# The second pass of a two-layer convolution block: normalisers, the last band's depthwise taps and the key sums in another order

## The chip, the cores and the metric

The kernel runs on one core of a Trainium2 chip. The metric is the time of one execution on the device, in microseconds. A median of three executions stands for a kernel, and a separate execution was recorded by the hardware profiler. The engines have these names in the profile: PE (TensorE, the matrix engine) and PEld (its weight loads), DVE (VectorE), ACT (ScalarE), POOL (GpSimd) and SP (SyncE, which issues most DMAs). Each engine runs its instructions in the order in which it was given them.

## The reference

Input x has 8 images of 384 channels and 64 × 64 tokens, in float32. Two layers follow each other, each with a residual (x becomes x + f(norm(x))) and each with a group normalisation of 32 groups per image in front of it.

- Layer 0 is linear attention. 1 × 1 convolutions give queries, keys and values. Queries and keys are rotated by token position and then sent through elu + 1. With 6 heads of 64 channels:

```
kv         = sum over tokens n of  k[n,d] * v[n,e]
k_sum      = sum over tokens n of  k[n,d]
out[n]     = q[n] · kv / (q[n] · k_sum + 1e-6)
layer0     = conv1x1(out, Wfc) + bfc
```

- Layer 1 is a convolutional feed-forward block. A 1 × 1 convolution is followed by a filter in the Fourier domain of every 8 × 8 block, then by a 3 × 3 depthwise convolution (zero padding), then by a gate, gelu(first half of the channels) times second half, and by a 1 × 1 convolution from 192 to 384 channels.

## The kernel before

**Tiling.** Channels lie on partitions in three tiles of 128. An image is cut into 8 bands of 512 tokens, which are 8 rows of 64. A band of an image, `x_b_j`, is loaded by SP (`load_x`), and layer 0 adds its result in place. It is stored after layer 0 (`store_x`), and POOL's queue later adds layer 1's output `y_b_j` to it in DRAM with an accumulating DMA (L845). Bands and `y` share a pool of 10 buffers, so that a load can wait for the `y` that had its buffer.

**Keys.** For each band `k_project` (matmuls pk, L438) and `v_project` (pv, L454, evicted by ACT at L461) make keys and values, and `accumulate` adds them over the tokens into one PSUM tile acc (L470; image 0 takes another form, L483).

**Second pass.** When an image's keys are complete, `queries` runs. Per band:
- `q_project` loads a table tq (SP) and does three groups of matmuls pq (L597). Then come the rotation (DVE L610, 625, 626, ACT L624) and elu + 1 (ACT L337, 338, DVE L339), which leave qc.
- `q_normalise` makes pn = q · k_sum (L635), then a chain of small steps in turn on DVE (L643, 644, 649, 651) and ACT (L648, 650): the reciprocal, split in two bf16 parts.
- `q_spread` spreads it over the channels (prb, L659, four PSUM tiles), and DVE multiplies qc by it (L668).
- `project_out` does pf (L676). DVE adds bias and residual (L680), and the sums for the next normalisation are taken on ACT and DVE.

At its start the heads' matrices are folded with the output weights (`finish`): kvt_bd on DVE (L571), pt (L583), pm (L508), mt (DVE L513). POOL copies k_sum into ks_bd (L498), which pn needs.

**Band loop.** After the second pass of image b its layer 1 runs band by band, and the keys of image b + 1 are made between its steps. `expand_filter` is pi (L694) and pd (L708), with the filter on DVE (tf, L716); `back_transform` is pb (L729), copied by ACT into a ring of two padded bands. The depthwise convolution is one ACT step (`first_taps`, L776) and eight DVE steps (`taps`, L788) per channel tile, 24 per band. `gate_taps` is L794 to L799, and `contract` is pw (L815, L826). The taps of a band run a band later, since they need the row below, and `contract` a band after that. So when image b + 1's second pass starts, bands 6 and 7 of layer 1 of image b aren't through: `before_last` contracts band 6, `gate` does the 24 taps and the gate of band 7, and `output` contracts band 7. These are called from inside `queries`, as is the chain for the next image's layer-0 normalisation and key weights (`layer0_chain(b + 1)`: small matmuls ps_m, ps_mc, ps_v, ps_r, and pbk).

**The last image** has no next keys. In bands where `on_array` holds, PE does the depthwise taps of channel tile 2 with diagonal matrices (ptap, L764), and DVE does 16 taps in place of 24.

**What sets the order.** The Python order of calls gives the order of work in outline, with generators that yield between matmul groups. A framework then schedules instructions on each engine and places the waits. There are eight PSUM buffers of 128 × 512, handed round by one pool, so a matmul group can also wait until an older tile in its buffer has been read. Two buffers hold taps.

The lines of `queries` around the normalisers and the last band's work before the change:

```
if j != 1:
    normaliser[j + 1] = q_normalise(b, j + 1, q[j + 1])
run(project)
...
q_spread(b, j, q[j], normaliser.pop(j))
if j == 0:
    gate()
```

Of the kernel before, what the change touches and what calls it, by code (L numbers as in the profile page):

```python
# [12 lines left out]
ALU = mybir.AluOpType  # L13
# [3 lines left out]
CT = 3  # L17
H = W = 64
N = H * W
NBAND = 8  # L20
# [97 lines left out]
def conv_blocks_kernel(ctx: ExitStack, tc: tile.TileContext, a: dict, out: bass.AP, nb: int):  # L118
    nc = tc.nc
# [20 lines left out]
    def load_x(b, j):  # L140
        if b >= nb:
            return
        t = xp.tile([P, CT, BT], F32, tag="x", name=f"x_{b}_{j}")
        nc.sync.dma_start(t, x_in[b][:, :, j * BT : (j + 1) * BT])
        xt[b, j] = t
# [484 lines left out]
    def q_normalise(b, j, q):  # L630

        pn = ps_tile(f"pn_{b}_{j}")
        for t in range(CT):
            for s in range(4):
                nc.tensor.matmul(  # L635
                    pn[32 * s : 32 * s + 32, :P],
                    ks_bd[:, t, :],
                    q[:, t, s * P : (s + 1) * P],
                    start=(t == 0),
                    stop=(t == CT - 1),  # L640
                )
        rn = small.tile([P, P], F32, tag="rn", name=f"rn_{b}_{j}")
        nc.vector.tensor_scalar_add(rn, pn[:, :P], 1e-6)  # L643
        nc.vector.reciprocal(rn, rn)

        part = small.tile([P, P], BF16, tag="part", name=f"part_{b}_{j}")
        parts = small.tile([P, P], BF16, tag="parts", name=f"parts_{b}_{j}")
        nc.scalar.copy(part, rn)  # L648
        nc.vector.scalar_tensor_tensor(rn, part, take_off[:, 0:1], rn, ALU.mult, ALU.add)
        nc.scalar.copy(part, rn)  # L650
        nc.vector.scalar_tensor_tensor(parts, part, take_off[:, 1:2], rn, ALU.mult, ALU.add)
        return parts
# [19 lines left out]
    def project_out(b, j, q, mt):  # L672
        for m in range(CT):
            p_ = ps_tile(f"pf_{b}_{j}_{m}")
            for t in range(CT):
                nc.tensor.matmul(  # L676
                    p_, mt[:, t, m * P : (m + 1) * P], q[:, t, :], start=(t == 0), stop=(t == CT - 1)
                )
            xm = xt[b, j][:, m, :]
            nc.vector.scalar_tensor_tensor(xm, p_, bfc[:, m : m + 1], xm, ALU.add, ALU.add)  # L680
            if m == 0:
                yield
        if j == 1:
            differences[b] = taps_pool.tile([P, CT, BT], F32, tag="dw", name=f"differences_{b}")
        band_sums(b, 1, j, xt[b, j], differences.get(b))
# [64 lines left out]

    def on_array(b, j):

        return b == nb - 1 and j in (3, NBAND - 2, NBAND - 1)

    def make_diagonals():
        t = small.tile([P, CT, C], F32, tag="wk", name="diagonals", bufs=1).rearrange("p t c -> p (t c)")
# [21 lines left out]
            dw_pe[b, j] = ps_tile(f"ptap_{b}_{j}")  # L778
            array_taps(b, j, range(9 if j == NBAND - 1 else 6))

    def taps(b, j):

        t, acc = ring[j % 2], dw[b, j]
        for m in range(CT - on_array(b, j)):
            for k in range(1, 9):
                src = t[:, m, k // 3 : k // 3 + 8, k % 3 : k % 3 + W]
                wd = w_dw[:, m, k : k + 1]
                nc.vector.scalar_tensor_tensor(acc[:, m], src, wd, acc[:, m], ALU.mult, ALU.add)  # L788

    def gate_taps(b, j):  # L790
        g = gated
# [9 lines left out]
    def depthwise_gate(b, j):  # L801
        taps(b, j)
        gate_taps(b, j)
# [43 lines left out]
    def contract(b, j):  # L847
        run(contraction(b, j))
# [14 lines left out]
    def chain_of(*chains):  # L863
        for c in chains:
            yield from c

    def run(*chains):

        chains = list(chains)
        while chains:  # L870
            chains = [c for c in chains if next(c, chains) is not chains]
# [62 lines left out]
                    sum_weight(self.wv, "wv")  # L934
                self.vbias = v_bias(self.b, self.params)

    def queries(b, keys, before_last, gate, output):


        wq, qbias = keys.wq, keys.qbias  # L940
        q, done = {}, []
        run(q_project(b, 0, wq, qbias, q))
        before_last()
        run(keys.accumulate(NBAND - 1))
        finish = keys.finish(done)
        for _ in zip(q_project(b, 1, wq, qbias, q), finish):
            pass
        prepared = []
        chain = layer0_chain(b + 1, prepared)
        normaliser = {0: q_normalise(b, 0, q[0])}  # L950
        for j in range(NBAND):

            if j < NBAND - 2:
                project = q_project(b, j + 2, wq, qbias, q)
                for _ in range(2 if j else CT):
                    next(project)
                if j == 0:
                    run(finish)
                    mt = done[0]
                if j != 1:  # L960
                    normaliser[j + 1] = q_normalise(b, j + 1, q[j + 1])
                run(project)
            if 2 <= j < NBAND - 2:
                next(chain, None)
            q_spread(b, j, q[j], normaliser.pop(j))
            if j == 0:
                gate()
            if j >= 1:
                output_ = project_out(b, j - 1, q.pop(j - 1), mt)
                if j in (1, NBAND - 2):  # L970
                    next(output_)
                    normaliser[j + 1] = q_normalise(b, j + 1, q[j + 1])
                run(output_)
                if j < NBAND - 2:
                    next(chain, None)
            if j == 2 and b < nb - 1:
                output()
            if j in (4, 5):
                load_x(b + 1, j - 4)
            if j == NBAND - 2:  # L980
                run(chain)
        run(project_out(b, NBAND - 1, q.pop(NBAND - 1), mt))
        return prepared

# [6 lines left out]
    prepared = []  # L991
    run(layer0_chain(0, prepared))
    keys = Keys(0, prepared)
# [4 lines left out]
    for c0, at, n in QRUNS:  # L998

        t, p0, quarter, first = at // P, at % P, c0 // QC, c0 % QC  # L1000
# [42 lines left out]
    def nothing():  # L1043
        pass

    before_last = gate = output = nothing
    for b in range(nb):
        prepared = queries(b, keys, before_last, gate, output)
        keys = Keys(b + 1, prepared)
        params = []  # L1050
        chain, more = norm_chain(b, 1, params), chain_of(keys.project_k(0), keys.load_values(), keys.project_k(1))
        last = b == nb - 1
        if last:

            more = contraction(b - 1, NBAND - 1) if b else iter(())
        for steps in (2, 0, 1, 1) if last else (2, 1, 1, 3):
            next(chain)
            for _ in range(steps):
                next(more, None)
        run(chain)  # L1060
        ahead = normalised(b, 0, params, (8, 8), "f")
        run(more)
        if last:
            break
        first_values = keys.project_v(0)
        next(first_values, None)
        for j in range(NBAND):
            if j < 2:
                fill = chain_of(keys.project_v(j) if j else first_values, keys.accumulate(j))
            else:  # L1070
                fill = chain_of(keys.project(j), keys.accumulate(j - 1 if j > 2 else NBAND))
            tf = []
            h = normalised(b, j, params, (8, 8), "f") if j else ahead
            store_x(b, j)
            if 1 <= j < NBAND - 1:
                load_x(b + 1, j + 1)
            layer1 = expand_filter(b, j, h, tf)
            items = 1 if j < 2 else 2

            def some(n):  # L1080
                for _ in range(n):
                    next(fill)

            next(layer1)
            some(items)
            run(layer1)
            some(2 * items)
            back_transform(b, j, tf[0])
            first_taps(b, j)
            some(items)  # L1090
            if j > 1:
                contract(b, j - 2)
            run(fill)
            keys.prepare(j)
            if j > 0:
                depthwise_gate(b, j - 1)
            stream_stats(b + 2, j)
        keys.prepare(NBAND)

        def before_last(b=b):  # L1100
            contract(b, NBAND - 2)

        def gate(b=b):
            depthwise_gate(b, NBAND - 1)

        def output(b=b):
            contract(b, NBAND - 1)


    make_diagonals()  # L1110
    b = nb - 1
    h = ahead
    for j in range(NBAND):
        tf = []
        layer1 = expand_filter(b, j, h, tf)
        run(layer1)
        store_x(b, j)
        if j < NBAND - 1:
            h = normalised(b, j + 1, params, (8, 8), "f")
        back_transform(b, j, tf[0])  # L1120
        if j and on_array(b, j - 1):

            array_taps(b, j - 1, range(6, 9))
        first_taps(b, j)
        if j >= 2:
            contract(b, j - 2)
        if j >= 1:
            taps(b, j - 1)
            gate_taps(b, j - 1)
# [45 lines left out]
```

## Time and profile before

| | |
|---|---|
| median of three executions | 3442.15 us (3442.06 to 3443.75) |
| profiled execution, own time | 3442.33 us |
| its span in the profile | 3440.6 us |
| mean granted PE clock | 0.989 |
| busy: PE, DVE, ACT, POOL | 3319.7, 2786.9, 1976.0, 143.2 us |
| chain that ended last, by engine | PE 76%, DVE 18%, ACT 4% |
| costliest group on DVE: taps, L788 | 1512 instructions, 1059.5 us |
| x load, y accumulate, tq load: issue to landing | 5.9, 7.8, 4.8 us |

The span is the time from the first to the last instruction that the profile holds, and the execution's own time is 1.73 us more. A busy time is the union of an engine's instructions; the rest of the span is idle. In lists of instructions the columns are start, duration, engine, line, operation, what it writes from what it reads, size and count of merged instructions. The bracket gives the idle time of that engine just before it and what ended it. A list of waits gives total, number and longest of them. "DVE qc L339" means: the DVE instruction of line 339 that writes qc. A matmul group's duration reaches to the modelled end of the last one, so groups overlap by a tenth or two; times per step in the text are spacings of starts.

### The profile page before, as it was taken

How to read it: one execution, taken by the hardware profiler on the slowest of the kernel's cores; microseconds unless marked ns; L12 is line 12 of the kernel's file. 1: busy time of each engine (PE TensorE's matmuls, PEld its weight loads, DVE VectorE, ACT ScalarE, POOL GpSimd, SP SyncE). 2: the span in 40 equal slices, each digit the busy share in tenths (PEclk: the TensorE clock that was granted, in tenths of full speed). 3: DMA queues.
4: the chain of work that ended last, by engine and by line, in shares of the span. 5: the costliest groups of instructions: out<-in, count | busy, mean ns of one | idle time of the engine just before them, and what ended most of it. 6: DMA issues, size and time to landing. Idle time of an engine off the chain costs nothing.

```text
span 3440.6 us, 53200 instructions
## 1 busy us (share of the span) xinstructions
PE 3319.7 (96%) x21374; PEld 1856.2 (54%) x21374; DVE 2786.9 (81%) x4430; ACT 1976.0 (57%) x3854; POOL 143.2 (4%) x247
## 2 busy tenths in 40 slices
PE   8999999999999999999999999989999899999987
PEld 5544565456654566445664456644566445664454
DVE  6587789868898688986889868897788977899597
ACT  4445666556664566555665556655576555555553
POOL 0000001000010000100001000010000000000000
PEclk9999999999999999999999999999999999999999
DMA  6323244332343333442343423334243331333112
GB/s 221 112 89 115 65 111 100 114 124 66 92 112 115 110 84 87 100 131 96 82 108 90 133 90 92 94 98 131 81 111 92 107 121 55 66 83 101 51 27 48
DMA packets 149484, 336.01 MB, mean 98 GB/s; under 512 B 27141, under 2 KB 38389, under 8 KB 141045
## 3 DMA queue, kind: packets, MB, share of 16 engines
q1 hardware_dynamic: 123844, 282.85, 24.5%
q0 software_dynamic: 25200, 49.55, 10.0%
q8 instruction: 168, 2.75, 0.3%
q14 instruction: 80, 0.65, 0.1%
q10 hardware_dynamic: 192, 0.21, 0.0%
HBM read 232.70 MB, written 99.88 MB: 97 GB/s over the span
## 4 chain that ended last, share of the span: by engine, by line
PE 76%; DVE 18%; ACT 4%; issue 1%; DMA 0%; SPq 0%; DVEq 0%; ACTq 0%
PE pi L694 14%; PE pk L438 13%; PE pf L676 13%; PE pv L454 12%; PE pq L597 7%; DVE dw L788 6%; PE pw L815 4%; PE pd L708 2%; PE pb L729 2%; PE pw L826 2%; PE acc L483 2%; PE acc L470 2%; DVE qc L339 1%; DVE qc L610 1%; ACT ring L739 1%
## 5 line engine op out<-in xcount | busy, mean ns | idle before, releaser
L788 DVE SCALAR_TENSOR_TENSOR dw<-ring,w_dw,dw 128x512 f32<-128x512 f32 x1512 | 1059.5, 749 | 262.5 <-ACT ring L745 223.9
L438 PE MATMUL pk<-wk,x 128*128 128x384 f32 x1536 | 545.0, 496 | 0.0
L676 PE MATMUL pf<-qc,mt 128*128 128x512 f32 x1152 | 518.8, 604 | 17.1 <-DVE qs L610 17.0
L597 PE MATMUL pq<-x,wq 128*128 128x512 f32 x1152 | 528.1, 607 | 0.1
L694 PE MATMUL pi<-w_in,hf 128*128 128x384 f32 x1536 | 516.1, 492 | 1.3 <-ACT hf L332 1.3
L454 PE MATMUL pv<-wv,x 128*128 128x384 f32 x1344 | 470.0, 488 | 0.0
L438 PEld LDWEIGHTS pk<-wk,x 128*128 128x128 f32 x1536 | 283.5, 191 | 205.3 <-issue 32.5
L694 PEld LDWEIGHTS pi<-w_in,hf 128*128 128x128 f32 x1536 | 287.8, 191 | 196.3 <-issue 4.6
L676 PEld LDWEIGHTS pf<-qc,mt 128*128 128x128 f32 x1152 | 214.8, 191 | 271.3 <-issue 231.8
L597 PEld LDWEIGHTS pq<-x,wq 128*128 128x128 f32 x1152 | 215.2, 193 | 255.8 <-issue 244.4
L454 PEld LDWEIGHTS pv<-wv,x 128*128 128x128 f32 x1344 | 253.6, 190 | 181.4 <-issue 8.4
L461 ACT COPY v<-pv 128x384 f32<-128x384 f32 x224 | 108.8, 486 | 417.8 <-PE pv L454 417.1
L680 DVE SCALAR_TENSOR_TENSOR x<-pf,bfc,x 128x512 f32<-128x512 f32 x192 | 141.1, 744 | 103.9 <-PE pf L676 103.2
L624 ACT ACTIVATE qs<-pq,qbias 64x512 f32<-64x512 f32 x128 | 87.6, 685 | 193.4 <-DVE qc L610 175.1
L701 ACT COPY ht<-pi 128x384 f32<-128x384 f32 x256 | 114.9, 484 | 114.7 <-PE pi L694 111.6
L815 PE MATMUL pw<-gated,w_out 128*128 128x256 f32 x768 | 177.5, 380 | 0.2 <-DVE gated L795 0.2
L441 DVE TENSOR_TENSOR kc<-pk,kbias 128x384 f32<-128x384 f32 x256 | 141.1, 551 | 40.9 <-PE pk L438 40.9
L337 ACT ACTIVATE qs<-qc 128x1536 f32<-128x1536 f32 x64 | 95.1, 1486 | 135.9 <-DVE qc L626 125.8
L845 POOL DMA_DIRECT2D out_dram<-y x63 | 80.7, 1281 | 2068.8 <-DVE dw L788 1047.8
L179 ACT ACTIVATE differences<-x,shift 128x512 f32<-128x512 f32 x168 | 120.2, 716 | 76.6 <-DVE x L680 76.6
L815 PEld LDWEIGHTS pw<-gated,w_out 128*128 128x128 f32 x768 | 145.0, 190 | 34.7 <-issue 5.7
L337 ACT ACTIVATE ks<-kc 128x1536 f32<-128x1536 f32 x64 | 95.2, 1487 | 100.9 <-DVE kc L445 72.0
(171 smaller groups left out, 4384.4 us busy)
## 6 DMA issues: line engine op xcount, KB each, us to landing
tq<-in_tq SPq DMA_DIRECT2D x64, 1024.0 KB, 4.8
x<-in_x SPq DMA_DIRECT2D x64, 768.0 KB, 5.9
tk<-in_tk SPq DMA_DIRECT2D x64, 768.0 KB, 4.4
out_dram<-x SPq DMA_DIRECT2D x63, 768.0 KB, 3.3
out_dram<-y POOLq DMA_DIRECT2D x63, 768.0 KB, 7.8
xs<-in_x SPq DMA_DIRECT2D x56, 768.0 KB, 5.9
wk<-in_wk SPq DMA_DIRECT2D x8, 576.0 KB, 3.8
wfc<-in_wfc SPq DMA_DIRECT2D x8, 576.0 KB, 7.7
```

The source lines that it names most:

```text
L179: nc.scalar.activation(out[:, m, :], x_[:, m, :], AF.Identity, bias=shift[:, m : m + 1], accum_out=of_m[0])
L337: nc.scalar.activation(e, x_, AF.Relu, scale=-1.0)
L438: nc.tensor.matmul(pk[:, :C], tokens(t), wks[:, t, :], start=(t == 0), stop=(t == CT - 1))
L441: nc.vector.tensor_add(kc[:, i, :], pk[:, :C], bias)
L454: nc.tensor.matmul(pv[:, :C], xt[b, j][:, t, i * P : (i + 1) * P], wvs[:, t, :], start=(t == 0), stop=(t == CT - 1),)
L597: nc.tensor.matmul(p_, wqs[:, t, m * P : (m + 1) * P], xt[b, j][:, t, :], start=(t == 0), stop=(t == CT - 1),)
L676: nc.tensor.matmul(p_, mt[:, t, m * P : (m + 1) * P], q[:, t, :], start=(t == 0), stop=(t == CT - 1))
L680: nc.vector.scalar_tensor_tensor(xm, p_, bfc[:, m : m + 1], xm, ALU.add, ALU.add)
L694: nc.tensor.matmul(p_[:, :C], h[:, t, i * P : (i + 1) * P], w_in[:, t, :], start=(t == 0), stop=(t == CT - 1),)
L701: nc.scalar.copy(ht[:, i, :], p_[:, :C])
L788: nc.vector.scalar_tensor_tensor(acc[:, m], src, wd, acc[:, m], ALU.mult, ALU.add)
L815: nc.tensor.matmul(p_[h][:, m - m0, :], w_out[:, 0, m * P : (m + 1) * P], gated[:, h * HT : (h + 1) * HT], start=(m == m0), stop=False,)
```

## The change

There are five parts.

1. The taps of one channel tile become a function, and the previous image's last band a generator, `last_band`: one tile's 8 taps in each of bands 2, 3 and 4 of the second pass, the gate with the third, the contraction in band 5. Before, all 24 taps and the gate were called in band 0, the contraction in band 2. In the last image's second pass the contraction is left to a later place in both kernels.
2. `queries` is written out anew. pn_1 comes after prb_0 and the first tile of pq_3, where it was right after the fold; pn_2 comes after prb_1, ahead of the second tile of pf_0. The chain's steps come up to a band later, and its rest after the loop. The loads of the next image's bands 0 and 1 come in bands 5 and 6, where they were in 4 and 5.
3. In the band loop every accumulation comes a band after its keys. Before, those of bands 0 and 1 came in their own band.
4. In the last image `on_array` holds for bands 6 and 7; before, also for band 3.
5. Band 6's last three array taps are issued in `taps`, after the contraction of band 5, where they were ahead of band 7's first taps.

```diff
     def on_array(b, j):
-        return b == nb - 1 and j in (3, NBAND - 2, NBAND - 1)
+        return b == nb - 1 and j >= NBAND - 2
...
+    def tile_taps(b, j, m):
+        t, acc = ring[j % 2], dw[b, j]
+        for k in range(1, 9):
+            src = t[:, m, k // 3 : k // 3 + 8, k % 3 : k % 3 + W]
+            wd = w_dw[:, m, k : k + 1]
+            nc.vector.scalar_tensor_tensor(acc[:, m], src, wd, acc[:, m], ALU.mult, ALU.add)
+
     def taps(b, j):
...
+        if on_array(b, j) and j < NBAND - 1:
+            array_taps(b, j, range(6, 9))
         for m in range(CT - on_array(b, j)):
...
+            tile_taps(b, j, m)
...
-    def queries(b, keys, before_last, gate, output):
+    def queries(b, keys, before_last, late):
...
-        normaliser = {0: q_normalise(b, 0, q[0])}
-        for j in range(NBAND):
-
+
+        normalise(0)
+        run(q_project(b, 2, wq, qbias, q))
+        run(finish)
+        mt = done[0]
+        q_spread(b, 0, q[0], normaliser.pop(0))
+        project = q_project(b, 3, wq, qbias, q)
+        next(project)
+        normalise(1)
+        run(project)
+        output_ = project_out(b, 0, q.pop(0), mt)
+        next(output_)
+        q_spread(b, 1, q[1], normaliser.pop(1))
+        normalise(2)
+        run(output_)
+        for j in range(2, NBAND):
             if j < NBAND - 2:
                 project = q_project(b, j + 2, wq, qbias, q)
-                for _ in range(2 if j else CT):
+                for _ in range(2):
                     next(project)
...
-                if j != 1:
-                    normaliser[j + 1] = q_normalise(b, j + 1, q[j + 1])
+                normalise(j + 1)
                 run(project)
-            if 2 <= j < NBAND - 2:
                 next(chain, None)
             q_spread(b, j, q[j], normaliser.pop(j))
-            if j == 0:
-                gate()
...
-            if j == 2 and b < nb - 1:
-                output()
-            if j in (4, 5):
-                load_x(b + 1, j - 4)
+            output_ = project_out(b, j - 1, q.pop(j - 1), mt)
             if j == NBAND - 2:
-                run(chain)
+                next(output_)
+                normalise(j + 1)
+            run(output_)
+            if j < NBAND - 2:
+                next(chain, None)
+            if j == 5:
+                load_x(b + 1, 0)
+            next(late, None)
+            if j == 6:
+                load_x(b + 1, 1)
+        run(chain)
...
+    def last_band(b):
+        for m in range(CT):
+            tile_taps(b, NBAND - 1, m)
+            if m == CT - 1:
+                gate_taps(b, NBAND - 1)
+            yield
+        if b + 1 < nb - 1:
+            contract(b, NBAND - 1)
...
-                fill = chain_of(keys.project_v(j) if j else first_values, keys.accumulate(j))
+                fill = chain_of(keys.project_v(j) if j else first_values, keys.accumulate(j - 1))
             else:
-                fill = chain_of(keys.project(j), keys.accumulate(j - 1 if j > 2 else NBAND))
+                fill = chain_of(keys.project(j), keys.accumulate(j - 1))
...
-                    next(fill)
+                    next(fill, None)
...
         back_transform(b, j, tf[0])
-        if j and on_array(b, j - 1):
-
-            array_taps(b, j - 1, range(6, 9))
         first_taps(b, j)
```

More of the change, by code (lines that the diff above doesn't have):

```diff
@@ L779, in first_taps @@
             array_taps(b, j, range(9 if j == NBAND - 1 else 6))
+    def tile_taps(b, j, m):
[4 more added lines that the diff above has]
+            nc.vector.scalar_tensor_tensor(acc[:, m], src, wd, acc[:, m], ALU.mult, ALU.add)
     def taps(b, j):
-        t, acc = ring[j % 2], dw[b, j]
+        if on_array(b, j) and j < NBAND - 1:
+            array_taps(b, j, range(6, 9))
         for m in range(CT - on_array(b, j)):
[L785 to L788, printed above, removed]
+            tile_taps(b, j, m)
     def gate_taps(b, j):
@@ L935, in prepare, with normalise @@
                 self.vbias = v_bias(self.b, self.params)
-    def queries(b, keys, before_last, gate, output):
+    def queries(b, keys, before_last, late):
         wq, qbias = keys.wq, keys.qbias
-        q, done = {}, []
+        q, done, normaliser = {}, [], {}
+        def normalise(j):
+            normaliser[j] = q_normalise(b, j, q[j])
         run(q_project(b, 0, wq, qbias, q))
@@ L949, in queries @@
         chain = layer0_chain(b + 1, prepared)
-        normaliser = {0: q_normalise(b, 0, q[0])}
-        for j in range(NBAND):
+        normalise(0)
[13 more added lines that the diff above has]
+        for j in range(2, NBAND):
             if j < NBAND - 2:
                 project = q_project(b, j + 2, wq, qbias, q)
-                for _ in range(2 if j else CT):
+                for _ in range(2):
                     next(project)
-                if j == 0:
-                    run(finish)
-                    mt = done[0]
-                if j != 1:
-                    normaliser[j + 1] = q_normalise(b, j + 1, q[j + 1])
+                normalise(j + 1)
                 run(project)
-            if 2 <= j < NBAND - 2:
                 next(chain, None)
             q_spread(b, j, q[j], normaliser.pop(j))
-            if j == 0:
-                gate()
[L968 to L975, printed above, removed]
-            if j == 2 and b < nb - 1:
-                output()
-            if j in (4, 5):
-                load_x(b + 1, j - 4)
-            if j == NBAND - 2:
-                run(chain)
+            output_ = project_out(b, j - 1, q.pop(j - 1), mt)
+            if j == NBAND - 2:
+                next(output_)
[9 more added lines that the diff above has]
+        run(chain)
         run(project_out(b, NBAND - 1, q.pop(NBAND - 1), mt))
@@ L1044, in nothing @@
         pass
-    before_last = gate = output = nothing
+    def last_band(b):
[6 more added lines that the diff above has]
+            contract(b, NBAND - 1)
+    before_last, late = nothing, iter(())
     for b in range(nb):
-        prepared = queries(b, keys, before_last, gate, output)
+        prepared = queries(b, keys, before_last, late)
         keys = Keys(b + 1, prepared)
@@ L1101, in before_last @@
             contract(b, NBAND - 2)
[L1103 to L1107, printed above, removed]
+        late = last_band(b)
     make_diagonals()
```

## The prediction

> **What bounds the kernel now.** I read the page's busy table first, then TensorE's waits, then the stage where those waits sit.
>
> ```profile
> PE 3319.7 (96%) x21374; PEld 1856.2 (54%) x21374; DVE 2786.9 (81%) x4430; ACT 1976.0 (57%) x3854; POOL 143.2 (4%) x247
> ```
>
> TensorE (PE) is idle for only 3440.6 − 3319.7 = 121 us, and no matmul of an image goes away, so this is nearly all that a reordering can win. The waits say on what PE stands:
>
> ```profile
> PE pn L635 <- DVE qc L339: 36.1, 20, 3.4
> PE pf L676 <- DVE qs L610: 17.0, 12, 1.8
> PE pb L729 <- DVE tf L716: 12.8, 7, 3.6
> PE pn L635 <- DVE qs L610: 7.9, 7, 2.3
> PE acc L470 <- ACT v L461: 6.9, 6, 1.1
> ```
>
> The normaliser (pn) and output projection (pf) lines, 36.1 + 17.0 + 7.9 = 61 us, all stand at the head of the second pass; pb is mostly the last image's. Windows of image 2 (columns: busy of PE, PE's weight loads, DVE, ACT, POOL, then clock, DMA share, GB/s) show that the other engine is then full:
>
> ```profile
> 1000.00:1060.00 60.00, 50.03 (x262) 22.39 (x257) 59.36 (x101) 30.35 (x42) 7.12 (x13) 0.97 0.31 89
> 1060.00:1120.00 60.00, 60.00 (x265) 28.53 (x266) 46.41 (x82) 32.44 (x63) 1.55 (x3) 1.00 0.47 144
> ```
>
> DVE works 59.36 of the first 60 us, then 46.41 of the next. So this is a short DVE-bound stretch before a PE-bound one. PE's timeline in it:
>
> ```profile
> 1011.16 1.05 PE L635 MATMUL pn<-qc,ks_bd 128*32 128x128 f32 x24 [0.96 <-DVE qc L339]
> 1012.14 7.99 PE L597 MATMUL pq<-x,wq 128*128 128x512 f32 x18
> 1019.97 2.10 PE L508 MATMUL pm<-wfc,kvt 128*128 128x384 f32 x6
> 1025.41 0.86 PE L635 MATMUL pn<-qc,ks_bd 128*32 128x128 f32 x24 [3.35 <-DVE qc L339]
> 1026.21 0.35 PE L659 MATMUL prb<-parts,expand 32*128 32x128 bf16 x12
> 1026.48 9.69 PE L597 MATMUL pq<-x,wq 128*128 128x512 f32 x18
> 1039.87 0.86 PE L635 MATMUL pn<-qc,ks_bd 128*32 128x128 f32 x24 [0.64 <-DVE qs L610]
> 1042.51 5.42 PE L676 MATMUL pf<-qc,mt 128*128 128x512 f32 x12 [1.78 <-DVE qs L610]
> 1054.41 0.86 PE L635 MATMUL pn<-qc,ks_bd 128*32 128x128 f32 x24 [1.34 <-DVE qc L339]
> 1059.93 7.99 PE L676 MATMUL pf<-qc,mt 128*128 128x512 f32 x18 [1.08 <-DVE qs L610]
> ```
>
> The brackets sum to 9.15 us; 0.5 of waits on kvt_bd just before and 0.17 on ps_m make 9.8. The pq group of 9.69 us, otherwise 7.9, ran partly at half clock: 1.77 us more. In the DVE timeline 16 of the 24 depthwise taps of the previous image's last band (L788) stand ahead of the elu (L339) for which pn_1 waits.
>
> **What the Trainium skill says.** "Perfetto Trace Analysis", Optimization Strategy, advises interleaving regimes when the most-contended engine changes over time; the two windows are that case. "TensorE: Matmul & The Clock Gate", Part 1, has the clock halve after at least one idle window of about 3.4 us, free-running. The trace agrees on the length (the low stretch is 3.41 us, from 1026.7), but the window before it was idle only some 2 us; the measurement decides, so I don't count gaps under 3.4 us as safe. "PSUM — Partial Sum Buffer", Specifications, gives eight banks per partition; no view shows banks, but the program has eight PSUM buffers, which decides my two new waits below.
>
> **The change, part by part** (durations are spacings in the timelines).
>
> *Last band's taps (24 × 0.66 = 15.8 us of DVE) and gate (0.6 + 2 × 0.45 = 1.5 us).* Nothing is removed. In the built order 12 taps instead of 16 now precede qc_1's elu, the other 12 and the gate follow in bands 2 to 5. DVE is thus 4 × 0.66 = 2.6 us earlier at that point, 1.26 at qc_0's elu. pn_0 hardly gains (0.3 us): POOL's ks_bd copies (L498) end at 1011.7, and their speed is untouched.
>
> *Normalisers.* pn_1 moves behind prb_0 and pq_3_0; pn_2 behind prb_1. What was queued behind pn_1's 3.35 us, the twelve prb and pq_3, goes ahead. I walked PE's new order from the same start (pq_0 at 987.04): pq_2 ends 1019.75, pm 1021.85, prb_0 1022.15. pq_3_0 now needs the buffer of pq_2_2, which ACT reads at L624 (behind its elu steps) until about 1023.6: **a new wait of 1.5 us**. pn_1 follows at 1026.35 without waiting. pq_3_1 needs a buffer of prb_0, which DVE reads at L668 until about 1029.1: **a new wait of 1.9 us**. pq_3 ends 1034.4, pf_0_0 1037.05; prb_1, pn_2 and the rest of pf_0 1043.6, pq_4's first two tiles 1048.9, pq_4 1052.5, prb_2 and pf_1 1060.6. Before, pf_1 ends at 1067.85 with 0.28 of a ps_m ahead of it that has now moved behind. So 1067.85 − 1060.6 − 0.28 ≈ **7.0 us per image**, 7 images with a predecessor: 49 us. The new waits can leave a half-clock stretch of up to 1.7 us; I take half, 0.85 × 7 = −6.
>
> *Bands 2 to 5.* There a band needs 13.2 us of DVE for its queries over 71/4 = 17.8; with 12 × 0.66 + 1.5 + 3 (layer 0's chain) = 12.4 more over four bands DVE is at (52.8 + 12.4)/71 = 92%. My walk shows no PE wait, since queries are projected two bands ahead, but DVE takes its work in order, and each late L610 holds a bank. From nothing to 3 us per image; I take 1 × 6 = −6.
>
> *contract(b,7) from band 2 to band 5.* 24 matmuls, 4.3 us of PE, all moved. Its y goes out by POOL's accumulate (7.8 us to landing). The load x_{b+1,1} takes y's buffer: issued near 1134, landing 5.9 later, 1140; pk_3_1 wants it near 1154. 13 us of cover, so nothing; without it the loss is one for one. The stores behind it on SP wait for later work anyway. x_{b+1,0} waits for an accumulate already landed: nothing.
>
> *Layer-0 chain half a band to a band later.* It ends before the keys that need wk; each small wait (0.17 to 0.3) sits elsewhere: nothing. If wk came late, pk would wait directly.
>
> *acc a band later.* In band 1 of the band loop acc stands 1.15 us on v (L461); the waits list has 6.9 us of it. The new acc_0 reads a v evicted a band earlier: **+7**. If that v were late too, the wait would return.
>
> *Image 0.* No taps precede it, PE is dense; the new bank wait costs about 0.9: **−1**.
>
> *Last image.*
>
> ```profile
> 3315.64 7.81 PE L764 MATMUL ptap<-ring,diagonals 128*128 128x512 f32 x12 [1.91 <-ACT ring L744]
> 3407.15 10.57 PE L764 MATMUL ptap<-ring,diagonals 128*128 128x512 f32 x24 [1.77 <-ACT ring L744]
> ```
>
> Band 3's tile 2 leaves the array: PE loses nine taps at (3417.56 − 3407.15)/12 = 0.87 us, where pw follows, 7.8 us in all, and the 1.91 wait, DVE gains 8 × 0.66 = 5.3, ACT one tap. Band 6's last three array taps now follow pw_5, so 3 × 0.87 = 2.6 us no longer stand between band 7's ring and its own nine. Here pb also waits for DVE's tf (2.04 and 2.50 near the end), so part of the 5.3 comes back. My walk has the end 4 to 6 us earlier; I take **+4.5**, bounds −5 (DVE sets the end throughout) and +9.7 (all of 7.8 and 1.91).
>
> Sum: 49 − 6 − 6 + 7 − 1 + 4.5 = 47.5 us. The profiled execution took 3442.33 (span plus 1.73), so 3394.8, and the median of 3442.15 lies 0.2 below: **3394.6 us**.
>
> **Rivals.** A difference from no change can be told from about 0.2% (7 us).
> *Waits only move.* The two new bank waits grow, and DVE at 92% makes others in bands 2 to 5, so that a third of the stage's 49 is left. For it: my walk already has 3.4 us of them, and DVE's work is only later, not less. Against: DVE has 13.6 us spare in the next 60. Then 7 + 4.5 − 1 + 16 = 26.5 → 3416.
> *Nothing of the second pass is won.* DVE's 120-us total bounds both windows: only acc and tail, 7 + 4.5 − 1 = 10.5 → 3432. Against: 105.8 of the 120 us are busy.
> *Slower: the last band's gate comes too late.* DVE, in order, runs it behind queries; y_7's accumulate lands after 1148, the load behind it on SP misses pk_3_1, and PE stops. It decides once y_7 slips more than 13 us against my walk; each us beyond costs one per image, six times. A slip of 25 costs 12 × 6 = 72, against the 47.5: 3467. For it: 92% leaves little to catch up. Against: a slip needs DVE over 100% for four bands.
> *The change does not do what it says:* the scheduler might hoist the spread taps again. It did hoist 12 of 24; taking it to 16 gives back about half of the stage, near 3416.
>
> **How the numbers follow.** Forecast near 3395 (its own range 3378 to 3408): 0.60. Waits move or taps hoisted, 3416: 0.20. Only acc and tail: 0.08. Slower, by the gate, the last image's −5 with clock losses, or new waits: 0.12. With no half clock and no wait in bands 2 to 5 (12 us) it is 3383, with the tail's upper bound (5 more) 3378. The range of 8 in 10 is 3374 to 3428. Faster 0.85 (the first three, less 0.03 near the bound), within 0.2% 0.05, slower 0.10.
>
> **What would show it.** Right: pn ← L339 falls from 36.1 to under 8 us; two new waits per image, pq on ACT's L624 and on DVE's L668, 1 to 2 us each; acc ← L461 gone; PE busy about as before less 8 to 14; image period from 419.7 to between 411.5 and 413.5; window 1060 to 1120 fuller on DVE, over 54. Wrong: pk waiting for x's DMA (the gate rival), pf or pq waiting on L610 in bands 2 to 5 over 2 us per image (DVE bound), low clock in each second pass, or tf late for pb throughout the last image.

## The result

The changed kernel takes 3386.34 us (median of 4 runs, 3383.77 to 3389.49), where the kernel before takes 3442.43 beside it. The ratio is 0.9837, with a 95% interval from 0.982 to 0.9854: 56 us faster. The forecast was 3394.6 with a range from 3374 to 3428, so the direction and the range held, and the gain was 8 us larger than the sum said. The profiled execution took 3384.08 us for a span of 3382.3.

The page's busy table of the changed kernel (columns as before):

```profile
PE 3300.6 (98%) x21356; PEld 1850.2 (55%) x21356; DVE 2786.1 (82%) x4438; ACT 1965.9 (58%) x3849; POOL 142.6 (4%) x247
```

PE's idle time fell from 121 to 3382.3 − 3300.6 = 82 us, and its busy time by 19 us. Some 8 of these are the nine array taps that are gone. The trace also has 53.7 us at half clock in place of 75.7; work at half speed takes twice as long, so up to 11 us of the rest is that (an estimate from these two figures). DVE works as long as before. PE's list of waits (total, times, longest) has new names at its head:

```profile
PE pq L597 <- ACT qs L624: 16.9, 7, 2.5
PE pb L729 <- DVE tf L716: 13.3, 7, 2.8
PE pq L597 <- DVE qc L668: 11.0, 7, 2.0
PE px L400 <- DMA x<-in_x: 7.2, 3, 6.4
PE pn L635 <- DVE qc L339: 6.8, 7, 1.0
```

The normaliser's wait on the elu (L339) went from 36.1 us to 6.8, those of pf and pn on L610 and that of acc on L461 are no longer in the list. In their place stand exactly the two that the forecast named: pq on L624 and on L668, once in each of seven images. The same stage of image 2 in PE's timeline:

```profile
1001.49 1.05 PE L635 MATMUL pn<-qc,ks_bd 128*32 128x128 f32 x24 [0.96 <-DVE qc L339]
1002.47 7.99 PE L597 MATMUL pq<-x,wq 128*128 128x512 f32 x18
1010.30 2.10 PE L508 MATMUL pm<-wfc,kvt 128*128 128x384 f32 x6
1012.33 0.44 PE L659 MATMUL prb<-parts,expand 32*128 32x128 bf16 x12
1015.26 2.84 PE L597 MATMUL pq<-x,wq 128*128 128x512 f32 x6 [2.50 <-ACT qs L624]
1018.04 0.86 PE L635 MATMUL pn<-qc,ks_bd 128*32 128x128 f32 x24
1020.94 7.11 PE L597 MATMUL pq<-x,wq 128*128 128x512 f32 x12 [2.04 <-DVE qc L668]
```

After these two waits PE's next one is 0.2 us at a ps_r in the band loop. The windows that answer to those shown of before, moved by the same distance from pq_0:

```profile
990.48:1050.48 60.00, 54.00 (x266) 24.18 (x262) 57.30 (x93) 29.00 (x40) 7.12 (x13) 0.97 0.39 121
1050.48:1110.48 60.00, 60.00 (x263) 27.73 (x261) 54.79 (x95) 36.58 (x69) 0.14 (x1) 1.00 0.29 98
```

DVE's crowded window fell from 59.36 to 57.30 and the next rose from 46.41 to 54.79, with PE full in it: this is the interleaving of the two stretches.

Where the 58.2 us of span went can be read from the start of one image's pq_0 to the next one's (before, after):

| part | before | after | gain |
|---|---|---|---|
| up to pq_0 of image 0 | 159.6 | 158.9 | 0.8 |
| image 0 | 407.75 | 406.36 | 1.4 |
| images 1 to 6, sum | 2516.9 | 2477.2 | 39.7 |
| image 7 to the end of its second pass | 154.5 | 149.6 | 5.0 |
| image 7, rest | 201.8 | 190.4 | 11.4 |

An image of the changed kernel takes 412.3 us (images 1, 3, 5 and 6) or 414.0 (2 and 4), against 419.7 (image 6: 418.5). The 1.7 us go with one stretch of half clock in the second pass. The second pass alone, from pq_0 to the end of the last pf, takes 163.9 us before and 158.7 after, as the mean of images 1 to 6. That is 31.5 of their 39.7 us; the other 8.2 lie in the band loop.

### The profile page after: what moved, and what is told of

The parts are those of the page before. It is cut to its first block, busy times and chain, and to the rows that moved or that the text cites. A ratio compares the mean times of both kernels' runs of the same rounds, so it can differ in the third digit from the quotient of the medians.

```text
span 3382.3 us, 53235 instructions
## 1 busy us (share of the span) xinstructions
PE 3300.6 (98%) x21356; PEld 1850.2 (55%) x21356; DVE 2786.1 (82%) x4438; ACT 1965.9 (58%) x3849; POOL 142.6 (4%) x247
## 4 chain that ended last, share of the span: by engine, by line
PE 82%; DVE 14%; ACT 2%; issue 1%; DMA 0%; SPq 0%; DVEq 0%; ACTq 0%
PE pf L676 15%; PE pk L438 14%; PE pi L694 13%; PE pv L454 13%; PE pq L597 9%; DVE dw L787 6%; PE pw L820 4%; PE pb L729 3%; PE pd L708 2%; PE pw L831 2%; PE acc L470 2%; PE acc L483 2%; PE pn L635 1%; DVE qc L610 1%; DVE qc L339 1%
## 5 line engine op out<-in xcount | busy, mean ns | idle before, releaser
L461 ACT COPY v<-pv 128x384 f32<-128x384 f32 x224 | 108.7, 485 | 423.9 <-PE pv L454 416.3
L624 ACT ACTIVATE qs<-pq,qbias 64x512 f32<-64x512 f32 x128 | 87.4, 683 | 123.8 <-DVE qc L610 122.6
```

## Experiments

Two theories were to be told apart. The first: the gain comes from DVE work (the last band's taps and gate) that leaves the crowded head of the second pass. The second: it comes from the normalisers' places on PE. Parts 3 to 5 of the change were measured on their own; the chain's steps and the loads of part 2 were not. The indented texts say what was expected of a run before it was built.

### The last band early again

```diff
         for m in range(CT):
             tile_taps(b, NBAND - 1, m)
-            if m == CT - 1:
-                gate_taps(b, NBAND - 1)
-            yield
+        gate_taps(b, NBAND - 1)
+        yield
...
         q_spread(b, 0, q[0], normaliser.pop(0))
+        next(late, None)
...
-            next(late, None)
+            if j == 2:
+                next(late, None)
```

> The changed kernel (3386 us) with the last band's 24 taps and gate called in band 0 of the second pass again and its contraction in band 2, the normalisers staying in their new places. If the gain of the second pass (6.2 us per image without the accumulation's 1.1) comes from DVE work taken out of its crowded head, 9 of the 24 taps and the gate, about 8 us of DVE, come back between the first elu steps and pf_0: nearly all is lost, 7 images x 5 to 6, 3420 to 3428. If it comes from the normalisers' places alone, 3384 to 3392. I expect most of it lost, 3415 to 3425.

It takes 3426.6 us (0.9953 of the kernel before, 0.9936 to 0.997): 40 us are lost, 5.8 per image on average. PE's timeline of it:

```profile
1022.74 4.54 PE L597 MATMUL pq<-x,wq 128*128 128x512 f32 x6 [2.49 <-ACT qs L624]
1027.20 0.86 PE L635 MATMUL pn<-qc,ks_bd 128*32 128x128 f32 x24
1028.41 5.42 PE L597 MATMUL pq<-x,wq 128*128 128x512 f32 x12 [0.35 <-DVE qc L668]
1037.55 0.35 PE L659 MATMUL prb<-parts,expand 32*128 32x128 bf16 x12 [1.14 <-DVE parts L651]
1040.20 1.51 PE L635 MATMUL pn<-qc,ks_bd 128*32 128x128 f32 x24 [2.30 <-DVE qs L610]
1053.88 0.86 PE L635 MATMUL pn<-qc,ks_bd 128*32 128x128 f32 x24 [0.73 <-DVE qc L339]
```

The waits are back, behind pn_1 instead of at it: DVE has eight taps and the gate between the elu of band 2 and the end of band 3's rotation, and the steps of the second normaliser (L643 to L651) stand among them. In the second passes of images 1 to 7 PE idles 61.9 us in place of 38.4, and half clock is granted for 47.8 us in place of 13.6, which is up to 17 us of PE's work (an estimate, half of the difference). These two make up the 40 us. The mean second pass of images 1 to 6 takes 164.5 us, no less than the 163.9 of the kernel before: new places for the normalisers don't help while this work stands there. The edit moves the contraction back too; in image 2's second pass PE has no wait of over 0.1 us behind those shown, so the contraction's place costs nothing there.

### The normalisers in their old places

```diff
-        q_spread(b, 0, q[0], normaliser.pop(0))
-        project = q_project(b, 3, wq, qbias, q)
-        next(project)
         normalise(1)
-        run(project)
+        q_spread(b, 0, q[0], normaliser.pop(0))
+        run(q_project(b, 3, wq, qbias, q))
+        q_spread(b, 1, q[1], normaliser.pop(1))
         output_ = project_out(b, 0, q.pop(0), mt)
         next(output_)
-        q_spread(b, 1, q[1], normaliser.pop(1))
         normalise(2)
```

> The changed kernel with pn_1 right after the fold again and pn_2 after the first pf_0, the taps staying spread. The elu for which pn_1 waits starts 36.3 us after the pass begins in the changed kernel and 36.5 before, so pn_1 would again stand some 3 us. If the normalisers' places make the gain, it is lost, 3415 to 3428; if the taps do, PE loses the 3 us at pn_1 but not the two new waits of 2.5 and 2.0 us on ACT L624 and DVE L668, since these buffers come free meanwhile: 3380 to 3392. I expect the second, up to 3395.

It takes 3398.2 us (0.9872, 0.9857 to 0.9886), 12 us more than the changed kernel, some 3 us above the range I gave. PE's waits in it:

```profile
PE pn L635 <- DVE qc L339: 29.5, 14, 3.4
PE pf L676 <- ACT y L845: 10.7, 6, 1.8
```

pn_1 stands 3.35 us on the elu as before, and neither L624 nor L668 is waited for. What was not foreseen is the second line: band 5's pf waits for ACT to move y out of the contraction's buffers, 1.8 us in six images. That the PSUM buffers are handed on in another order is the likely reason; no view shows the buffers. With this wait PE idles 44.7 us in the second passes of images 1 to 7, in place of 38.4, and half clock is granted for 30.7 us in place of 13.6, up to 8.5 us of PE's work (an estimate, as above).

The four orders side by side, as the mean second pass of images 1 to 6, in us:

| | normalisers in their old places | in their new places |
|---|---|---|
| taps and gate early | 163.9 (before) | 164.5 |
| taps and gate spread | 160.7 | 158.7 (changed) |

So the first theory holds for the larger part: spreading the taps wins 3.2 us per image with the old places and 5.8 with the new ones. The new places win 2.0, and only once the taps are spread. The kernel before also differs from the others in the places of the chain and of two loads.

### Accumulation a band later, alone

```diff
-                fill = chain_of(keys.project_v(j) if j else first_values, keys.accumulate(j))
+                fill = chain_of(keys.project_v(j) if j else first_values, keys.accumulate(j - 1))
             else:
-                fill = chain_of(keys.project(j), keys.accumulate(j - 1 if j > 2 else NBAND))
+                fill = chain_of(keys.project(j), keys.accumulate(j - 1))
```

This is made in the kernel before, and the filling loop passes over an empty chain.

> The kernel before with the accumulations of bands 0 and 1 a band later and nothing else. If v, a band old by then, is always there, the 1.15 us of PE at acc go in six images: 6.9 us, 3435 to 3436. If the second pass stays DVE-bound, so that PE's gain in the band loop is only waited off in front of pn, no change, 3441 to 3443.

It takes 3433.0 us against 3442.9 (0.9973, 0.9963 to 0.9983), 9.9 us less where 6.9 were expected. The wait on L461 is gone. An image takes 418.10 us in place of 419.68, 1.15 us of which are that wait. The other 0.4 us appear in image 6 as well, which had no such wait, and in the band loops of the changed kernel; their cause stays open.

### Band 3 of the last image, alone and undone

```diff
-        return b == nb - 1 and j in (3, NBAND - 2, NBAND - 1)
+        return b == nb - 1 and j >= NBAND - 2
```

> The kernel before with band 3 of the last image off the array and nothing else. In the forecast PE's nine taps (7.8 us), its 1.9 us wait and DVE's 5.3 us more made 4.5 with the other tail edit, this one some 2 to 3: 3439 to 3440. The traces say more: from band 3's to band 4's first matmul 30.8 us before and 20.4 after, 10.3 less, of which bands 4 and 5 give back 2. Then 8 us, 3433 to 3435, with band 3's stretch of half clock (10.2 us from 3310) gone in the trace.

This edit in the kernel before gives 3432.7 us (0.997, 0.9957 to 0.9982), 10.2 less. The reverse, in the changed kernel:

> The changed kernel with band 3 of the last image back on the array, DVE's 8 taps of its tile 2 again PE's nine. If band 3 off the array is what shortened the last image's end by more than forecast, it is 8 us slower than the changed kernel, 3393 to 3396, and the trace shows a stretch of half clock around band 3's array taps. If the array taps were dear only through the half clock that the old phase of waits brought, the cost is 3 to 5 us, 3389 to 3391.

It takes 3398.0 us, 11.7 more than the changed kernel. In both directions the edit is worth 10 to 12 us by the medians, where the two traces had promised 8 and the forecast 2 to 3. In the profiled executions the last image, from the end of its second pass on, is 8.4 us shorter in the first case and 13.0 longer in the second. PE's timeline of the last one, at band 3:

```profile
3262.51 1.85 PE L729 MATMUL pb<-idft,tf 64*64 64x64 f32 x48 [3.58 <-DVE tf L716]
3264.93 1.56 PE L729 MATMUL pb<-idft,tf 64*64 64x64 f32 x48 [0.58 <-DVE tf L716]
3268.39 7.79 PE L764 MATMUL ptap<-ring,diagonals 128*128 128x512 f32 x12 [1.91 <-ACT ring L744]
```

PE is idle for 6 us around this band's back transform, the granted clock is then halved for three windows (10.2 us) and the array taps run in it: six taps take 7.6 us, 1.27 each, not 0.87. From band 3's first pi to band 4's it is 30.7 us; with the taps on DVE it is 20.4 in the changed kernel, 21.0 in the edited old one. The half clock isn't gone in the edited old kernel, though: from band 3 on, leaving out the stretch that runs past the end, it has five stretches of 3.4 us where the kernel before had two that together last as long, 17.1 us. From band 3's first pi to the end it has 6.0 us less of PE busy and 2.1 less of PE idle.

### The array taps' order, alone

In the kernel before, the last three taps of an array band are issued after the contraction ahead of them, as in part 5; the lines are those of the change.

> The kernel before with each array band's last three taps issued after the contraction ahead of it instead of ahead of the next band's first taps, for bands 3 and 6. Forecast: three taps of 0.87 us leave the way from band 7's ring to its nine, 2.6 us, 3439 to 3440. If DVE's taps set the last bands, PE only waits at another place, 3442. The traces have band 6 to band 7 and the end together 4.3 us shorter after the change.

It takes 3442.4 us (0.9999, 0.9991 to 1.0007): no difference. In its profile band 7 has nine taps where it had twelve, but they take 9.69 us: a half-clock stretch fell on them. Whether 2.6 us are won at full clock this doesn't show. For the kernel before it is worth nothing that can be measured; in the changed kernel it was not undone alone.

### The price of a late y

```diff
-            next(late, None)
-            if j == 6:
+            if j < 5 or j == NBAND - 1:
+                next(late, None)
+            if j == NBAND - 1:
                 load_x(b + 1, 1)
```

> The changed kernel with the last band's contraction in band 7 in place of 5, and the load of the next image's band 1, which takes y's buffer, behind it. This prices the rival 'the gate comes too late'. In the changed kernel that load lands at 1127.2 and its first matmul is at 1146.7: 19.5 us of cover, where the forecast had 13. The contraction moves from 1107.9 to about 1129.5, so the load slips by 21 to 22: with 19.5 of cover PE stops 2 us per image, six times, 3396 to 3402. With the forecast's 13 it would be 8 per image, 3435. If the cover is larger than the trace shows, no change, 3384 to 3389.

It takes 3426.5 us (0.9953, 0.9938 to 0.9968): 40 us are lost, not 12. The load of x does come at the edge of its cover, but another transfer is hit first. The engines' timelines of it:

```profile
1146.25 0.43 SPq L909 DMA_DIRECT2D wv<-in_wv  x1
1153.09 0.75 DVE L352 TENSOR_SCALAR wv<-wv,rs 128x384 f32<-128x384 f32 x2 [5.41 <-DMA wv<-in_wv]
1154.50 1.41 PE L281 MATMUL ps_mc<-gm,of_group 32*128 32x1 f32 x6 [3.97 <-DVE gm L291]
```

On SP the load of wv stands behind that of x, which waits 12.1 us for y to land (at 1145.6) and is issued at 1145.77. wv's buffer comes free with the end of pf_7: in the changed kernel it is issued 0.2 us after that (1137.37), here 2.2 us (1146.25, pf_7 ending at 1144.08), and from issue to scaling it takes 6.8 us beside x's own transfer, where it took 4.5. DVE therefore stands 5.41 us at the scaling, in place of 1.12, and behind it is the small copy gm for which PE waits 3.97 us. The same scaling in the changed kernel:

```profile
1141.90 0.75 DVE L352 TENSOR_SCALAR wv<-wv,rs 128x384 f32<-128x384 f32 x2 [1.12 <-DMA wv<-in_wv]
```

Half clock follows, 6.8 us per image. The rival's mechanism is real, but its victim was not the one named: the forecast named only stores behind x on SP. By this reading x may slip by some 15 us, to the end of pf_7; in this one case 1.7 us beyond that went with a loss of 6.7 us per image.

### A better order

DVE's products L668 stood behind the mt copies of the fold. Three more kernels change that and then the place of the contraction. The first is called e8 in the later texts:

```diff
-        run(finish)
-        mt = done[0]
         q_spread(b, 0, q[0], normaliser.pop(0))
+        run(finish)
+        mt = done[0]
```

> The changed kernel with prb_0 and its product issued ahead of the fold's pm and mt copies, so that DVE's L668 no longer stands behind four mt copies (0.56 us each). If the new wait of 2.0 us of pq_3's second tile is due to those copies, it goes: 7 x 2.0 = 14 us, and fewer half-clock stretches follow, 3366 to 3374. If mt then comes late for pf_0, the wait only moves there and the time stays at 3382 to 3390. The 2.5 us wait on ACT L624 stays in both cases.

This takes 3374.8 us (0.9803, 0.9789 to 0.9818), just above the range I gave. The wait on L668 shrinks to 0.2 us and that on L624 goes. The second is against what I expected: pq_3's first tile now waits for L668, so it seems to have another buffer. No image's second pass has a half-clock stretch any more. Two waits are new, at prb_1 on the normaliser's last step and at band 5 on the eviction of y:

```profile
PE pf L676 <- ACT y L845: 10.1, 6, 1.7
PE prb L659 <- DVE parts L651: 9.7, 8, 1.4
```

The first of these lines is as in the kernel with the old normalisers. In e8 the last band's contraction is then put inside pf_4:

```diff
+            if j == 5:
+                next(output_)
+                next(late, None)
             run(output_)
...
-            next(late, None)
+            if j != 5:
+                next(late, None)
```

> The kernel of e8 (prb_0 ahead of the fold, 3374.8 us) with the last band's contraction between the first and second tile of pf_4 in place of after pf_4. In e8 PE waits 1.7 us per image for ACT's eviction of y (L845) before pf_5, six times 10.1 us: the buffers handed on by pw. If the wait is only one of places, pf_4's last two tiles (5.3 us) cover the eviction and it goes: 3364 to 3367. If pf_4's second tile itself now needs a buffer of pw, the wait comes earlier and is as long: 3373 to 3377.

That takes 3365.6 us (0.9774, 0.9758 to 0.979), as expected if places alone make the wait: pf_4's last tiles cover the eviction. The wait on y's eviction is gone from PE's list. It is the fastest kernel of this study, 78 us below the kernel before. One step further, the contraction ahead of band 5's query projection:

> The kernel of e8 with the last band's contraction ahead of band 5's query projection (after pf_3). If the wait on y's eviction is one of places, pq_7 covers it and it goes: 3364 to 3367. Against it: the gate must be done 8 us earlier, and DVE runs its last taps among band 4's queries. If the gate is late there, PE waits at pw for DVE's L804, up to 4 us per image: 3375 to 3400.

That takes 3420.9 us (0.9934, 0.9919 to 0.9949): worse than I gave it, by another way than the gate. Its waits show at pn of band 7 (5.4 us in image 2, 7.0 at most, on L339), and half clock is granted for 3.4 to 6.8 us in the second pass of each of images 1 to 6, where e8 had none. DVE's timeline shows why it waits:

```profile
1123.54 0.42 DVE L352 TENSOR_SCALAR wq<-wq,rs 128x384 f32<-128x384 f32 x1 [6.40 <-DMA wq<-in_wq]
```

Here the loads of wq stand on SP behind the second load of x: pq_7 ends at 1110.6, x is issued at 1116.25, after 7.3 us of waiting for y to land, and wq from 1116.71. In the fastest kernel wq is issued at 1095.04, ahead of both loads of x (1098.38 and 1115.79). It is the same failure as that of the late y, with another weight.

## Why the prediction was right, point by point

**The head of the second pass.** Forecast: 49 us of stage, less 6 for half clock and 6 for bands 2 to 5, so 37. The second passes are 31.5 us shorter in images 1 to 6 and 5.0 in image 7: 36.5. That the sum is so near is partly luck, since single terms were off and cancelled. The two new waits are 2.50 and 2.04 us, not 1.5 and 1.9, so that an image without half clock wins 5.8 us, not 7.0. Bands 2 to 5 cost nothing; no PE wait stands there, though DVE is at 55.7 of 60 us between 60 and 120 us after pq_0. Half clock cost 1.7 us in two of the six images 1 to 6 of the profiled execution, not half of it in each. The four runs lie 5.7 us apart, which is three to four such stretches; that these explain the spread is argued, since only one execution is profiled.

**What of the working failed.** The forecast counted 12 of the last band's taps ahead of the elu of band 1, where there were 16, and so had DVE 2.6 us earlier there. The trace has 15 ahead of it, and the step starts 36.3 us after pq_0, where it was 36.5. In both kernels it follows ACT's exponential (L338) within 0.03 us; the taps ahead of it fill a pause of DVE. The eight taps and the gate that stood *behind* this elu, and have left, are what counts, as their return shows. The forecast also took PE's 121 us of idle time for nearly all that can be won; 19 of the 58 us of span came out of PE's busy time.

**pf_1's end.** The walk had it 73.6 us after pq_0. It is 76.4 in image 2, and the two waits' excess (1.1) and one half-clock stretch (1.7) are the whole difference.

**acc.** The 6.9 us of wait are gone as forecast. The edit alone was worth 9.9; the other 3 us were in no term and are not explained.

**Image 0.** Forecast −1. Its second pass grew by only 0.2 us; the band loop fell by 1.6, as with the acc edit alone. The new buffer wait doesn't show there.

**The last image's end.** This is the term that was mis-sized: +4.5 with an upper bound of 9.7, and it measured 11.4. The single edits say where, though they don't add up. In the profiled executions this part of the kernel, 201.8 us before, takes 193.4 with band 3 off the array alone, 202.3 with the taps' order alone and 190.4 with both. Half clock fell on band 6 for 6.8, 3.4, 10.2 and 0 us of these; that this makes the 3 us between band 3 alone and both is argued, not shown. The forecast priced the taps at full clock (5.2 us for the six in that band's step), where they took 7.6; it let DVE's 5.3 us come back nearly whole, where bands 4 and 5 together grew by 2.2 us; and it left out the shorter waits for tf at that band, 4.2 us in two parts before and 2.8 after.

**The rivals.** Waits that only move: they moved, but from 9.2 us per image to 5.5 (the brackets shown). The taps were hoisted in part again: 15 of 24 stand ahead of that elu, not 12, but nine and the gate stay spread, and that was enough. The late gate has its cover, some 15 us where 13 were named, and beyond it the one case measured cost more than one for one, through wv.

## What to carry to other kernels

Where one engine is full for a while and has room a little later, take the work that has no deadline there out of the stretch; a new order on the waiting engine alone moves its waits. Before a load is delayed, list every load behind it on the same issuing queue and the in-order engine that consumes each of them: twice here a weight behind x, scaled by DVE, cost more than x itself. And price matrix work next to a wait at half clock, if the profile shows half clock in that place, but look where the half clock goes when that work is moved: in one kernel here as much of it came back later.

## What was not expected of the hardware

The halved clock lasts 3.41 us or a multiple of it, and it followed windows of that length in which PE had been idle only some 2 us (in the second pass of the changed kernel, 2.01 to 2.14 us before a halving, 1.90 and less before none). This is no sharp limit: in the last image of the same kernel 1.40 us stood before a halving. One stretch went with 1.7 us more in images 2 and 4. Where PE waits afterwards anyway it costs nothing: image 5 of the changed kernel had such a stretch, with 4.4 us of idle time in its second pass in place of 6.0, and took 412.32 us like images without one. In the kernel with the late y all of images 1 to 6 had one, and their second passes took 158.2 us, as did those of the changed kernel without one (158.1).
